# Cross-attention with image prompts: the last batch re-planned over eight PSUM banks, with a block diagonal prompt product

## The chip, the cores and the metric

The kernel runs on one core of a Trainium2 chip. The core has a matmul engine (TensorE, "PE" in the profile; its weight loads are "PEld"), a vector engine (VectorE, "DVE"), a scalar engine (ScalarE, "ACT"), a general engine (GpSimd, "POOL") and a queue that issues DMAs (SyncE, "SP"). PE writes into PSUM, a small memory of eight banks; DVE and ACT read it, POOL cannot. Each engine works through its own instructions in the order in which they are written, and engines wait for each other through semaphores. The metric is the device time of one execution in microseconds (us); lower is better. All arithmetic is fp32.

## What is computed

Eight batches; 112 queries of 320 channels each (20 heads of 16); a context of 375 tokens of 512 channels, of which the first 371 are text and the last 4 are image prompts. The reference, cut to what matters:

```python
text_ehs, ip_ehs = ehs[:, :-4], ehs[:, -4:]
q = heads(x @ W_q); k_t = heads(text_ehs @ W_k); v_t = heads(text_ehs @ W_v)
probs_t = softmax(q @ k_t.T * 0.25)                  # 112 x 371 per head
text_out = probs_t @ v_t
k_ip = heads(ip_ehs @ W_k_ip); v_ip = heads(ip_ehs @ W_v_ip)
qsem = l2norm(probs_t @ text_ehs)                    # 112 x 512 per head
sem = qsem @ l2norm(ip_ehs).T                        # 112 x 4
probs_ip = softmax(q @ k_ip.T * 0.25 + 0.5 * sem) * spatial_mask[:, None]
out = (text_out + probs_ip @ v_ip) @ W_out + b_out + x
```

The norm of `probs_t @ text_ehs` is the costly part. The kernel never forms that 112 x 512 product. It forms the Gram matrix of the context once per batch and needs, per head, the quadratic form of the probabilities with it.

## The kernel before, in words

**Groups.** The 20 heads of a batch b make five groups g of four heads. For one group, `multiplied` (L574) multiplies the transposed probabilities `xgT` of four heads with `u` on PE, in 12 steps j; the four heads use four row strips of PE at the same time. `u` holds the Gram matrix (half of it, doubled), the normalised prompts, a column of ones and, in its last 16 columns, the values of the group's heads. The result `ps_qd` is one PSUM bank per head: 371 columns of the Gram product, and 21 columns with the prompt products, the softmax sum and the text output.

**Around it.** `scores` (L528) makes one head's scores on PE into a bank `ps_s`. `probabilities` (L549) takes their negated maximum on DVE (`nmx`, L553), the exponential on ACT (`p`, L557) and sends p to `xg` by DMA (L560). `transposed` (L564) turns `xg` into `xgT` with one DVE instruction per group. `value_sums` (L597) copies the 21 columns to `pvs` on ACT. `reduced` (L626) multiplies the 371 columns with p and sums them on DVE (L630) into `ss`. `shared` (L602) does that for two of a group's four heads on ACT and POOL instead. `placed` (L502) copies the next group's values into `u` on POOL, in three pieces c; piece c may be written when PE has done the steps of the group in hand that read it. Scores are made two groups ahead (`LEAD`, L766).

**finish** (L643) ends a batch. It is a generator whose pieces are placed by hand between the groups of the next batch: `z`, `rn` (L672, L674); square root on ACT, then the table for Exp is loaded again (L677, L678), `zr` and the normalised text output `attn` (L680, L683); `fu`, the prompts' logits less their maximum (L688 to L694); `ex` (L698); `w`, the prompts' weights (L704 to L708); `wv`, the product of weights and prompt values `vip` on POOL, summed over four prompts and added to `attn` (L712 to L725); three transposes of `attn` into `ps_a` and the copy `aT` (L731, L735); the projection `ps_o` with W_out (L744); `ob`, the addition of x and bias (L753); the DMA to the output (L756). `ob` has one buffer. The last batch is finished in two parts, its first 16 heads (`first`) and its last four (`last`, with the sums on DVE, L720, L721).

**Other work between groups**, in `between` (L778): the Gram matrix, values, keys and queries of the next batches. `values` (L458) is 320 columns wide for the first and the last batch and 384 for the others, whose extra 64 columns are the keys of the last four heads, copied to `k3`; `keys` (L431) then makes its third block by three transposes of `k3` instead of four matmuls. `prompt_logits` (L510) makes `ps_ip`, the prompts' scores.

**PSUM.** Three pools share the eight banks: four for `ps_qd`, two for `ps_sc`, two for `ps_mm` (L78 to L80). `bank()` (L82) takes one of `ps_mm`, or of `ps_sc` with `spare`. A tile gets a bank when all readers of the bank's last tile are done.

**Order.** On PE, SP, DVE and ACT (and on POOL in the last batch) the instructions stand in the order of the program. The loop of L875 does batches 0 to 6, the loop of L930 the last batch, b = 7. What follows the loop (L974 to L985) interleaves the rest of batch 6 and the two parts of batch 7. `awake` (L364) gives PE matmuls whose results nobody reads. DMAs with tensors on chip are issued by SP, in order.

Of the kernel before, what the change touches and what calls it, by code (L numbers as in the profile page):

```python
# [20 lines left out]
def kernel(  # L21
# [174 lines left out]
    vipd = dram.tile([N, C], F32, tag="vipd", name="vipd", bufs=1)  # L196

# [233 lines left out]
    def keys(b):  # L431
        s = st[b]
        for i in range(NC):
            ps = bank(f"ps_k_{b}_{i}")
            if 0 < b < B - 1 and i == FULL:
# [22 lines left out]
    def values(b):  # L458
        s = st[b]
        ctxT, vext = s["ctxT"], s["vext"]  # L460
        w = C + REST if 0 < b < B - 1 else C
# [39 lines left out]

    def placed(b, g):  # L502

        s = st[b]
        for c in range(NT):
            nc.gpsimd.tensor_copy(  # L506
                region(b, c)[:, :, UV - c * P :], s["vr"][:, c * QN : (c + 1) * QN, g, :]
            )

    def prompt_logits(b):  # L510
        s = st[b]
        qT, _, j = queries[b]
        ps = bank(f"ps_ip_{b}", spare=b == B - 1)
# [14 lines left out]
    def scores(b, g, a, early=False):  # L528
# [6 lines left out]
        elif b == B - 1 and g > 1 and a < 2:  # L535

            ps = bank(f"ps_s_{b}_{g}_{a}")
        else:
            ps = ps_sc.tile([P, 512], F32, tag="sc", name=f"ps_s_{b}_{g}_{a}")
# [34 lines left out]
    def multiplied(b, g):  # L574
# [3 lines left out]
        for a in range(GROUP):  # L578

            if b == B - 1 and (g, a // 2) in ((NG - 2, 0), (NG - 1, 1)):  # L580
                banks.append(bank(f"ps_qd_{b}_{g}_{a}"))
# [15 lines left out]
    def value_sums(b, g):  # L597
        s = st[b]
        for h, ps in zip(groups[g], s["qd", g]):
            nc.scalar.copy(s["pvs"][:, h, :], ps[:S, TT:UW])  # L600

    def shared(b, g):  # L602
# [3 lines left out]
        if b == B - 1:  # L606
            t = work.tile([P, NE, TP], F32, tag="ctxT", name=f"shared_{b}_{g}")
            prods = [t[:S, a, :TT] for a, _ in some]
        else:

            t = work.tile([S, NIP, H, D], F32, tag="wv", name=f"shared_{b}_{g}", bufs=1)
            prods = [t.rearrange("p n h d -> p (n h d)")[:, a * TP : a * TP + TT] for a, _ in some]
        p = s["p", g]
        for a, (h, ps) in some:
            nc.scalar.copy(prods[a], ps[:S, :TT])
# [27 lines left out]
    def finish(b, heads=(0, H), eng=None, late=False, table=None):  # L643
# [55 lines left out]
        if table:  # L699
            nc.scalar.preload_act_table(table)  # L700
# [9 lines left out]

        wv = work.tile([S, NIP, H, D], F32, tag="wv", name=f"wv_{b}_{h0}", bufs=1)[:, :, :n]
# [16 lines left out]
        i0, i1 = h0 * D // P, -(-h1 * D // P)  # L728
# [11 lines left out]
        if not late:  # L740
            s["o"] = bank(f"ps_o_{b}", spare=b >= B - 2)
# [5 lines left out]
        if h1 < H:  # L747
            yield
            return
        yield  # L750

        ob = work.tile([S, C], F32, tag="ob", name=f"ob_{b}", bufs=1)
        nc.vector.tensor_tensor(ob, ps[:S, :C], s["xb"], ALU.add)  # L753
        yield

        nc.sync.dma_start(out[b], ob)  # L756
        del st[b]
# [20 lines left out]
    def between(b, g):  # L778
# [26 lines left out]
        if g == 3:  # L805
# [4 lines left out]
            run(("t", b), lambda: prompt_logits(b))  # L810
            if nb < B - 1:
# [5 lines left out]
        if g == 4:  # L817
# [6 lines left out]
            for bs in (first if b > 0 else []) + rest:  # L824
                run(("q", bs[0]), None)

# [48 lines left out]
    for n, (b, g) in enumerate(steps[:-NG]):  # L875
# [35 lines left out]
        if g == NG - 1:  # L911
# [17 lines left out]
    before = ("f", b - 1)  # L929
    for g in range(NG):  # L930
        coming = g + LEAD if g + LEAD < NG else None
        for j, _ in enumerate(multiplied(b, g)):
            for a in {0: (2, 3), 1: (0, 1)}.get(j, ()) if coming else ():
                scores(b, coming, a)
                probabilities(b, coming, a)
# [3 lines left out]
            if g == 2:  # L939
                run(before, lambda: finish(b - 1))  # L940
            if g == 3:
                nc.scalar.preload_act_table(AF.Sqrt)
            if g + 1 < NG:
                transposed(b, g + 1)
            if g == 2:
                run(before, None)
            if g == 3:
                run(before, None)
        value_sums(b, g)
        if g < LEAD + 1:  # L950
            sums = shared(b, g)
            next(sums)
            reduced(b, g, 2)
        else:
            reduced(b, g)
        if g + 1 < NG:
            placed(b, g + 1)
        if g < LEAD + 1:
            next(sums)
        if g == 0:  # L960
            run(("k", b), None)
            run(("f", b - 2), None)
        if g == 1:
            prompt_values(b)
        if g == 2:
# [63 lines left out]
```

## Time and profile before

| | us |
|---|---|
| median of 3 runs | 455.98 (454.32 to 457.4) |
| the profiled execution: device time | 457.81 |
| the profiled execution: span | 456.0 |
| PE busy, its share of the span | 440.5, 97% |
| DVE busy, its share | 312.5, 69% |
| first matmul of the last batch's five groups | 401.23, 409.27, 415.79, 424.35, 432.47 |
| the last `ob` ends | 453.02 |

How to read it: every row of a timeline has a start, a duration, an engine and a line; rows that follow each other are merged (x10). In brackets stands how long the engine had been idle before the row and who released it. Matmuls are pipelined, so what a matmul costs in a stream is read from the distance of two starts. An fp32 matmul of the program appears as two MATMUL rows, a transpose as one. Up to the start of the last batch PE has no gaps worth naming; the last 55 us are where PE, DVE, POOL and ACT wait for each other.

### The profile page before, as it was taken

To read this page: it belongs to the slowest core of one execution; us is meant where nothing else is said; L and a number is where in the kernel's file an instruction comes from. 1 tells how busy PE (TensorE), PEld (TensorE's weight loads), DVE (VectorE), ACT (ScalarE), POOL (GpSimd) and SP (SyncE) were. 2 spreads that over 40 slices of the span, in tenths; PEclk is the share of its full clock that TensorE was granted. 3 is DMA by queue.
4 is the path that set the end of the run, shared out by engine and by line. 5 is a ranking of instruction groups with operands and counts; after the bars stand their busy time and mean duration, and the time that the engine had idled before them with its cause. 6 is when DMAs were issued, how large, how long until landed. Compare 5 with 4: busy or idle time off the path is not lost.

```text
span 456.0 us, 12969 instructions
## 1 busy us (share of the span) xinstructions
PE 440.5 (97%) x5136; PEld 340.8 (75%) x5136; DVE 312.5 (69%) x657; ACT 190.4 (42%) x529; POOL 115.2 (25%) x264
## 2 busy tenths in 40 slices
PE   8998999999999999999999999999999999999885
PEld 8757867877678877887778877887768777877763
DVE  3047456786677668786676668787687668878883
ACT  2263233345344353345334353335335353356640
POOL 4302200102051114212061113312050213333490
PEclk9999999999999999999999999999999999999887
DMA  8679853645646454646645554545645455654100
GB/s 242 166 181 257 201 154 105 153 125 162 161 129 164 137 134 139 149 129 166 170 115 153 153 148 135 139 134 156 169 124 131 129 126 147 153 165 133 40 1 25
DMA packets 52069, 64.99 MB, mean 143 GB/s; under 512 B 18369, under 2 KB 43985, under 8 KB 52009
## 3 DMA queue, kind: packets, MB, share of 16 engines
q1 hardware_dynamic: 51568, 63.62, 52.5%
q8 instruction: 40, 0.66, 0.7%
q10 hardware_dynamic: 440, 0.56, 0.4%
q14 instruction: 21, 0.16, 0.1%
HBM read 19.46 MB, written 5.12 MB: 54 GB/s over the span
## 4 chain that ended last, share of the span: by engine, by line
PE 89%; DVE 3%; ACT 3%; issue 2%; DMA 1%; POOL 1%; SPq 0%; DVEq 0%; ACTq 0%; POOLq 0%
PE ps_qd L587 41%; PE ps_v L465 14%; PE ps_k L448 9%; PE ps_g L412 8%; PE ps_s L540 4%; PE ps_o L744 3%; PE ps_q L301 3%; PE ps_c L351 2%; PE ps_g L384 1%; PE ps_w L371 1%; ACT p L557 1%; DMA xg<-p 1%; PE ps_ip L517 1%; DVE xgT L568 1%; DMA ct<-in_ctx_dram 1%
## 5 line engine op out<-in xcount | busy, mean ns | idle before, releaser
L587 PE MATMUL ps_qd<-u,xgT 32*112 32x232 f32 (+11 forms) x3840 | 220.5, 354 | 4.4 <-POOL u L506 3.3
L587 PEld LDWEIGHTS ps_qd<-u,xgT 32*112 32x112 f32 x3840 | 185.1, 173 | 40.9 <-issue 9.5
L553 DVE TENSOR_REDUCE nmx<-ps_s 112x1 f32<-112x371 f32 x160 | 77.5, 528 | 75.6 <-PE ps_s L540 75.4
L568 DVE STREAM_TRANSPOSE xgT<-xg 128x1536 f32<-128x1536 f32 x40 | 118.9, 2973 | 4.8 <-DMA xg<-p 4.8
L557 ACT ACTIVATE p<-ps_s,nmx 112x371 f32<-112x371 f32 x160 | 82.5, 573 | 60.5 <-DVE nmx L553 48.1
L630 DVE CUSTOM_DVE_ANT_0 junk<-ps_qd,p 112x371 f32<-112x371 f32 x152 | 82.3, 542 | 18.3 <-ACT pvs L600 2.1
L506 POOL COPY u<-vr 128x64 f32<-128x64 f32 x120 | 26.0, 239 | 174.3 <-PE ps_qd L587 118.1
L540 PE MATMUL ps_s<-kT,qm 32*112 32x371 f32 x320 | 63.3, 476 | 0.4 <-ACT p L557 0.4
L465 PE MATMUL ps_v<-wv_sb,ctxT 128*128 128x384 f32 (+1 forms) x192 | 63.5, 480 | 0.0
L465 PEld LDWEIGHTS ps_v<-wv_sb,ctxT 128*128 128x128 f32 x192 | 35.2, 190 | 19.7
L448 PE MATMUL ps_k<-ctxT,wk_sb 128*128 128x371 f32 x144 | 48.7, 482 | 0.0
L600 ACT COPY pvs<-ps_qd 112x21 f32<-112x21 f32 x160 | 16.5, 189 | 66.6 <-PE ps_qd L587 66.5
L448 PEld LDWEIGHTS ps_k<-ctxT,wk_sb 128*128 128x128 f32 x144 | 26.5, 190 | 16.1 <-issue 0.5
L412 PE MATMUL ps_g<-ctxT 128*128 128x375 f32 (+2 forms) x168 | 37.4, 379 | 0.0
L412 PEld LDWEIGHTS ps_g<-ctxT 128*128 128x128 f32 x168 | 28.1, 190 | 8.4
L540 PEld LDWEIGHTS ps_s<-kT,qm 32*112 32x112 f32 x320 | 25.6, 170 | 5.0 <-ACT kT L455 2.1
L310 DVE TENSOR_SCALAR qm<-ps_q,emask 128x224 f32<-128x224 f32 (+1 forms) x25 | 9.2, 400 | 24.6 <-PE ps_q L301 24.5
L712 POOL TENSOR_TENSOR wv<-vip,w 112x1280 f32<-112x1280 f32 (+1 forms) x8 | 19.2, 2405 | 14.8 <-DVE w L708 14.6
L472 ACT COPY vext<-ps_v 128x384 f32<-128x384 f32 (+1 forms) x24 | 11.2, 466 | 27.1 <-PE ps_v L465 26.7
L455 ACT COPY kT<-ps_k 128x371 f32<-128x371 f32 x18 | 8.4, 469 | 28.9 <-PE ps_k L448 28.9
L744 PE MATMUL ps_o<-wo_sb,aT 128*112 128x320 f32 x48 | 16.4, 479 | 2.8 <-ACT aT L735 2.8
L400 ACT ACTIVATE ug<-ps_g 128x375 f32<-128x375 f32 (+2 forms) x24 | 9.0, 377 | 23.7 <-PE ps_g L412 20.6
(110 smaller groups left out, 324.1 us busy)
## 6 DMA issues: line engine op xcount, KB each, us to landing
xg<-p SPq DMA_DIRECT2D x160, 162.3 KB
u<-ug SPq DMA_DIRECT2D x128, 99.0 KB
vip<-vipd SPq DMA_DIRECT2D x8, 560.0 KB
ct<-in_ctx_dram SPq DMA_DIRECT2D x16, 256.0 KB
vr<-vd SPq DMA_DIRECT2D x32, 120.0 KB
vd<-vext SPq DMA_DIRECT2D x7, 320.0 KB
ct<-in_ctx_dram SPq DMA_DIRECT2D x8, 224.0 KB
vd<-vext SPq DMA_DIRECT2D x7, 160.0 KB
```

The lines of the kernel that those rows point to most:

```text
L412: nc.tensor.matmul(ps[:, : T - t0], ctxT[:, e, t0 : t0 + P], ctxT[:, e, t0:T], start=(e == 0), stop=(e == NE - 1),)
L448: nc.tensor.matmul(ps[:, :TT], wk_sb[:, e, i * P : (i + 1) * P], s["ctxT"][:, e, :TT], start=(e == 0), stop=(e == NE - 1),)
L465: nc.tensor.matmul(ps[:, :w], ctxT[:, e, c * P : (c + 1) * P], wv_sb[:, e, :w], start=(e == 0), stop=(e == NE - 1),)
L506: nc.gpsimd.tensor_copy(region(b, c)[:, :, UV - c * P :], s["vr"][:, c * QN : (c + 1) * QN, g, :])
L540: nc.tensor.matmul(ps[:S, :TT], qm[a * RG : (a + 1) * RG, i, r, j * S : (j + 1) * S], s["kT"][a * RG : (a + 1) * RG, i, :], start=True, st ...
L553: nc.vector.tensor_reduce(nmx, ps[:S, :TT], AX.X, ALU.max, negate=True)
L557: nc.scalar.activation(p, ps[:S, :TT], AF.Exp, bias=nmx)
L568: nc.vector.transpose(xT.rearrange("p j (k q) -> p q j k", q=QN), xg.rearrange("p q (j k) -> p q j k", k=RG),)
L587: nc.tensor.matmul(banks[a][:S, j * RG : UW], xT[a * RG : (a + 1) * RG, j, :S], region(b, c)[a * RG : (a + 1) * RG, q, q * RG :], start=(j ...
L630: nc.vector.tensor_tensor_reduce(out=junk, in0=ps[:S, :TT], in1=s["p", g][:, a, :], scale=1.0, scalar=0.0, op0=ALU.mult, op1=ALU.add, accu ...
L712: eng.tensor_tensor(wv, s["vip"][:, :, part], w.rearrange("p h n -> p n h").unsqueeze(3).to_broadcast([S, NIP, n, D]), ALU.mult,)
L744: nc.tensor.matmul(ps[:S, :C], aT[:, i, :], wo_sb[:, i, :], start=(i == 0), stop=(i == NC - 1))
```

## The change

1. **Batch 7's keys and values** follow the other batches: `values(7)` is 384 wide and the third key block is three transposes. These now stand in batch 6's group 3, where the other batches have theirs; the four matmuls of `ps_k` between groups 0 and 1 of the last batch go.
2. **`prompt_logits(7)`** moves from between groups 3 and 4 of the last batch to directly ahead of its group 0, behind the last `ps_q`.
3. **Banks and scores of the last batch.** The products of groups 1 to 4 and the scores for groups 2 to 4 change places among the three pools, so that the next tile takes a bank that comes free early. In groups 1 and 2 the scores of heads 0 and 1 are made at step j = 2 instead of j = 1. On ACT the two shared heads' copies come first (`pvs`, `shared`, `pvs`, `shared`), then the other two `pvs`.
4. **finish(6)** is later in its parts: its square root stands behind group 2's copies, its `fu` behind the transposition for group 4, its `w` behind group 3's reductions, and its transposes and projection behind group 4's products. `finish(7, first)` is re-ordered likewise: `ex` behind group 4's copies, `w` behind group 4's reductions.
5. **Prompt values by TensorE.** For batch 6 and for the first 16 heads of batch 7 the POOL work of L712 to L725 goes. The prompts' values are written once to DRAM as 80 rows (head, prompt) of 320 channels (`vipx`), loaded as `bd`, and two `affine_select`s on POOL zero the channels that are not the row's head, which makes a block diagonal matrix. `w` is transposed on PE (`wT`), and `ps_a` is the sum of `attn` times the identity and `bd` times `wT`, six matmuls for three transposes.
6. `awake(11)` becomes `awake(3)` and stands behind batch 6's projection; both `ob` additions stand at the end.

The diff, cut to its core:

```diff
+    vipx = dram.tile([2, H, NIP, C], F32, tag="vipx", name="vipx", bufs=1)
...
-            if 0 < b < B - 1 and i == FULL:
+            if b > 0 and i == FULL:
...
-        w = C + REST if 0 < b < B - 1 else C
+        w = C + REST if b > 0 else C
...
+    def prompt_values_by_head():
+        nc.sync.dma_start(vipx, vipd[N - 2 * NIP :, :].rearrange("(b n) c -> b n c", n=NIP)
+            .unsqueeze(1).to_broadcast([2, H, NIP, C]))
+    def load_prompt_values_by_head():
+        bd = io.tile([P, NT, E], F32, tag="ct", name="bd")[:HN, :2, :CP]
+        nc.sync.dma_start(bd[:, :, :C], vipx.rearrange("b h n c -> (h n) b c"))
+        return bd
+    def own_channels(bd):
+        nc.gpsimd.memset(bd[:, :, C:], 0.0)
+        v = bd[:, :, :C].rearrange("p b (h d) -> p b h d", d=D)
+        for sign, base in ((1, 0), (-1, NIP - 1)):
+            nc.gpsimd.affine_select(out=v, in_=v, compare_op=ALU.is_ge, fill=0.0, base=base,
+                pattern=[[0, 2], [-sign * NIP, H], [0, D]], channel_multiplier=sign)
...
-        ps = bank(f"ps_ip_{b}", spare=b == B - 1)
+        ps = bank(f"ps_ip_{b}")
...
-            if b == B - 1 and (g, a // 2) in ((NG - 2, 0), (NG - 1, 1)):
-                banks.append(bank(f"ps_qd_{b}_{g}_{a}"))
+            if b == B - 1 and (g, a // 2) in ((1, 0), (2, 1), (3, 1), (4, 1)):
+                banks.append(bank(f"ps_qd_{b}_{g}_{a}", spare=g == 3))
...
         for a, (h, ps) in some:                      # in shared()
+            if b == B - 1:
+                nc.scalar.copy(s["pvs"][:, h, :], ps[:S, TT:UW])
             nc.scalar.copy(prods[a], ps[:S, :TT])
...
+        if bd is not None:                           # in finish(), behind w
+            ps = ps_qd.tile([P, 512], F32, tag="qd", name=f"ps_wT_{b}")
+            nc.tensor.transpose(ps[: n * NIP, :S], w.rearrange("s h n -> s (h n)"), ident[:S, :S])
+            wT = work.tile([P, NE, TP], F32, tag="ctxT", name=f"wT_{b}")[:, 0, :S]
+            nc.scalar.copy(wT[: n * NIP], ps[: n * NIP, :S])
+            yield
+            ps = bank(f"ps_a_{b}_{h0}")
+            for i in range(i0, i1):
+                o = ps[:, i * S : (i + 1) * S]
+                nc.tensor.matmul(o, attn[:, i * P : (i + 1) * P], ident[:S, :S], start=True, stop=False)
+                nc.tensor.matmul(o, bd[: n * NIP, i * P : (i + 1) * P], wT[: n * NIP], start=False, stop=True)
...
-                run(("k", nb), None, 1)
+            if nb == B - 1:                          # end of between(6, 4)
+                run(("t", nb), lambda: prompt_logits(nb))
...
+        if (b, g) == (B - 3, 1): prompt_values_by_head()
+        if (b, g) == (B - 2, 1): bd = load_prompt_values_by_head()
-        if g == NG - 1:
+        if g == NG - 1 and b < B - 2:
             prompt_values(b)
...
+    places = {0: {0: (2, 3), 1: (0, 1)}, 1: {0: (2, 3), 2: (0, 1)}, 2: {0: (2, 3), 2: (0, 1)}}
     for g in range(NG):                              # the last batch
+        own = {}
+        for a in (0, 1) if g in places else ():
+            if g == 0: own[a] = bank(f"ps_s_{b}_{g + LEAD}_{a}")
+            elif g == 2: own[a] = ps_qd.tile([P, 512], F32, tag="qd", name=f"ps_s_{b}_{g + LEAD}_{a}")
...
+        if g <= LEAD:
+            sums = shared(b, g); next(sums); value_sums(b, g, 2); reduced(b, g, 2)
+        else:
+            value_sums(b, g)
+            if g == NG - 1:
+                run(before, None)                    # wT of batch 6
+                next(first)                          # ex of batch 7, first 16 heads
+                run(before, None)                    # ps_a and aT of batch 6
+                nc.scalar.preload_act_table(AF.Sqrt)
+                run(before, None)                    # ps_o of batch 6
+            reduced(b, g)
...
-        if g == 0:
-            run(("k", b), None)
         if g == 1:
             prompt_values(b)
+            own_channels(bd)
...
     last = finish(b, (FULL * HC, H), nc.vector, late=True)
-    run(before, None, 2)
-    awake(11, end=True)
-    for _ in range(3): next(last)
-    run(before, None)
-    next(first); next(last); next(first)
-    run(before, None)
-    drain(first); drain(last)
+    next(last)
+    next(first)                                      # w of the first 16 heads
+    next(last)
+    awake(3, end=True)
+    next(first)                                      # wT
+    for _ in range(2): next(last)                    # fu, ex of the last four heads
+    for _ in range(2): next(first)                   # ps_a, ps_o
+    for _ in range(4): next(last)
+    drain(gens[before]); drain(first); drain(last)
```

## The prediction

> **What bounds the kernel now.** I read the page's busy table and slices first.
>
> ```profile
> PE 440.5 (97%) x5136; PEld 340.8 (75%) x5136; DVE 312.5 (69%) x657; ACT 190.4 (42%) x529; POOL 115.2 (25%) x264
> ...
> PE   8998999999999999999999999999999999999885
> ...
> PEclk9999999999999999999999999999999999999887
> ```
>
> PE sets the time until the last batch; only the last slices have idle PE and a lower granted clock. So I then read the timeline of the last batch.
>
> ```profile
> 401.23 1.22 PE L587 MATMUL ps_qd<-u,xgT 32*112 32x392 f32 x10
> ...
> 401.70 0.25 ACT L313 COPY qT<-ps_q 128x112 f32<-128x112 f32 x1 [0.70 <-DVE qm L310]
> ...
> 404.62 3.03 DVE L568 STREAM_TRANSPOSE xgT<-xg 128x1536 f32<-128x1536 f32 x1
> ...
> 406.58 2.76 PE L448 MATMUL ps_k<-ctxT,wk_sb 128*128 128x371 f32 x8
> ...
> 409.27 1.22 PE L587 MATMUL ps_qd<-u,xgT 32*112 32x392 f32 x10
> ...
> 412.67 2.97 DVE L568 STREAM_TRANSPOSE xgT<-xg 128x1536 f32<-128x1536 f32 x1
> ...
> 415.79 1.57 PE L587 MATMUL ps_qd<-u,xgT 32*112 32x392 f32 x9 [1.09 <-DVE xgT L568]
> ...
> 417.44 0.85 POOL L668 TENSOR_TENSOR xb<-x_sb,bias_sb 112x320 f32<-112x320 f32 x1
> ...
> 423.37 0.74 POOL L683 TENSOR_TENSOR attn<-pvs,zr 112x320 f32<-112x320 f32 x1 [5.08 <-DVE zr L680]
> 424.06 0.58 POOL L506 COPY u<-vr 128x64 f32<-128x64 f32 x3
> ...
> 424.35 7.50 PE L587 MATMUL ps_qd<-u,xgT 32*112 32x392 f32 x96 [2.16 <-POOL u L506]
> ```
>
> Here DVE, not PE, paces. A group's products take PE 5.4 us (401.23 to 406.58). DVE waits 1.6 us for the first scores, takes their four maxima (about 1.9) and then transposes 3.0: the next `xgT` is there 6.4 us after the group's start, in both group 0 and group 1. In group 0 the `ps_k` matmuls fill the gap; ahead of group 2 PE idles 1.09, ahead of group 3 2.16, there for POOL, whose `u` stands behind `attn`, which waits for DVE's `zr`. Third, the stages of the end with busy times by engine (PE, PEld, DVE, ACT, POOL, how many instructions in brackets); the third number from the right is the granted clock. And the chain of waits:
>
> ```profile
> 424.30:426.40 2.10, 2.05 (x19) 1.42 (x23) 1.45 (x6) 1.24 (x7) 1.47 (x4) 1.00 0.03 8
> 426.40:429.80 3.40, 3.40 (x35) 3.38 (x31) 3.30 (x5) 1.66 (x6) 1.00 (x2) 0.50 0.01 2
> 438.00:440.00 2.00, 0.54 (x4) 0.30 (x3) 1.15 (x4) 1.61 (x4) 1.78 (x4) 1.00 0.00 0
> 440.00:446.90 6.90, 6.17 (x20) 4.86 (x21) 5.05 (x18) 2.17 (x7) 4.53 (x4) 0.51 0.02 7
> ```
>
> ```profile
> 438.63 1.28 ACT L700
> 439.93 0.41 ACT pvs L600 x4
> ...
> 440.73 3.54 PE ps_o L744 x6
> 444.27 3.75 PE ps_w L371 x22
> ...
> 448.50 0.23 ACT ex L698
> ...
> 452.53 0.49 DVE ob L753
> ```
>
> After each longer gap PE runs at half clock, for 3.4 and for 6.9 us. In the end the last four heads' `ex` waits for ACT's `aT`, thus for 22 slow matmuls of `awake`.
>
> **The change part by part**, against this execution (span 456.0, device time 457.81, the median 1.83 lower; I add the difference to the median).
>
> *Ahead of the last batch, PE-bound, so all of it counts.* Values: 8 matmul rows of 384 columns take 2.68 (328.82 to 331.50), of 320 columns 2.25 (379.02 to 381.27): +0.43 x 3 = **+1.29**. Third key block: three transposes, 0.36 in batch 5 (343.37 to 343.73), and a wait for the `kT` copy, which frees the bank: in batch 6 PE would be there at 392.33, the copy ends at 392.48: **+0.53** in all. `ps_ip`: six rows, 0.52 (391.81 to 392.33); but its third block needs the `qT` copy, which ended at 401.95 behind `qm`, while `ps_q` was issued by 401.13; group 0 is queued behind it on PE. Start of group 0 at about 402.2 instead of 401.23: **+1.0**. Group 0 so starts at 401.23 + 2.82 = 404.05. The two DMAs of the prompt values are two issues on SP (0.5 us, as `vip`'s) between issues of `xg` that wait for ACT anyway; uncovered they would cost 0.5 each. A DMA of `vip` goes as well.
>
> *Groups 0 to 2.* `ps_k` (2.69, and 0.52 of issue behind it) goes, but the next `xgT` is late instead: group 1 at 404.05 + 6.42 + 0.15 = 410.6 (before 409.27). ACT's reordered copies free both shared banks 1.1 us after group 0's end, by 410.5, in time; the DVE reductions that free the others end at 412.0, ahead of the scores at j = 2. Group 2 again 6.52 later: 417.15 (before 415.79). So the new banks take away little: DVE's order is as long as it was. Group 3: the 0.4 us that group 2's scores waited for a bank go; `xgT` ends at about 417.15 + 6.8 = 423.9. POOL: `attn` is behind the next `shared`, but memset and two selects come ahead of `xb` and `u`. The only row of a select is 0.29 for 128 columns, the lower end; POOL's 640-element product (1.56, L723) is the nearest row of that size, twice it the upper end. 0.29 x 5 = 1.46 lies at the product: I take 1.5 each. `shared` ends at 418.7; + 0.2 + 3.0 + 0.85 + 0.25 = 423.0: hidden behind `xgT`. From 2.0 each it shows; at 3.1 each group 3 starts 2.2 late, which costs the end 0.2, as PE has 1.9 to spare there (below). Group 3 at **424.05** (before 424.35): nearly all that was won is spent on the 2.82.
>
> *Groups 3, 4.* DVE now does two reductions and `xgT` ahead of `fu`: 423.9 + 1.6 + 2.95 + 1.35 = 429.8; on ACT `ex` 0.27 and the square root's table 1.28 stand ahead of group 3's `pvs`: 431.45; first reduction at 431.7 (before 431.94). PE may lose 1.9 here to half clock and still be in time. From there: four reductions, `z`, `rn` (to 434.6), `zr`, `sx`, `rx`, `w` (1.1 more), then `fu`, whose rows were 0.92, 0.90 and 0.65 beside POOL's `wv` work and 0.35, 0.24, 0.24 in the mean without: 437.2 (before 438.26). `pvs` of group 4 are no longer behind `ex` and a table load: reductions from **437.3** (before 440.13), 2.8 us won.
>
> *The end.* Three things take it back. (a) `ps_a` of batch 6 gets the bank of group 4's third head, so it waits for the third reduction: 439.3. `aT`, and behind `aT` on ACT the table for the square root, wait with it; before, that table was loaded early (L700). PE has idled 4 us and is at half clock: 12 rows at 0.19 (112/128 of the 0.214 between two slow `ps_w`; at full clock 0.10, by the 0.11 between two fast ones) + 0.3: 441.9; `aT` to 442.4; table 1.28, root, table 1.28: 445.2 (before 444.91). (b) PE: `ps_o` 3.33 as before, slow, six `ps_w` 1.28, `wT` 0.3, its copy on ACT 0.25: `ex` from 447.6 to 447.85 (before 448.72). (c) Behind `ex` DVE takes 2.16 to `attn`, as before, then batch 6's `ob` 0.49 (its bank is wanted by the last transpose); the last `ob` has to wait until that tile has been sent. Sending took from 453.02 to 455.04: 447.85 + 2.16 + 0.49 + 2.07 + 0.49 = 453.06, against 453.02. With the clock back at 445.5 (half of `ps_o` to `wT` 0.7 shorter) 452.4. I take 452.7: **−0.3**, and 455.98 − 0.3 = **455.7**.
>
> One rule weighs on this. Rows: PE idled 1.35 of the 3.4 us up to 426.4 and 1.3 of the 3.4 up to 440.0, and was halved after both; 1.09 of 412.7 to 416.1 left the clock alone. The Trainium skill, "TensorE: Matmul & The Clock Gate", section "Why this matters for your kernels", asks only for no gap above about 3 us. By it the new gaps of 1.1 to 1.45 us ahead of groups 1 to 3 are free; by the rows they lie at the edge. That is the slow rival below.
>
> **Rivals.**
> *PE stays warm at the end.* If the clock does not fall before 439.3 (its steps are 3.4 us apart, and the idle time began at 435.2): `aT` at 441.2, `ex` waits only for ACT's tables: 444.5. End 3.3 earlier, **452.6**. It decides where the 3.4 us steps fall: for it, one place in five; against it, 4 us of idle, twice what sufficed before. Only with a `ps_ip` that does not wait (1.0 less, which DVE hands on) does it come to 451.6, at the bound of 1% (451.4).
> *Slower: half clock in a group that makes scores.* Gaps of 1.2 ahead of group 1 and 1.1 ahead of group 2 now stand without `ps_k` as filler. It decides from somewhere between 1.09 and 1.3 us of idle PE in a 3.4 us stretch. A slow stretch brings that group's scores, and so DVE's whole order, 1.6 later (half of 3.4, less what falls behind the scores). One hit with the end at half clock throughout (last `ps_a` to `ps_o`, +1.5): 455.98 + 1.6 + 1.5 = **459.1**; two hits 460.7.
> *The banks do not do what they say*: scores wait for DVE as before, 0.4 once or twice: 456.3, the forecast's neighbourhood.
>
> **How the numbers follow.** No change as forecast: 0.48; banks that do nothing: 0.06. Warm end: 0.20, of which 0.13 with gains that no row shows, below 451.4. Slow stretches: 0.26, of which 0.19 with two hits or waits that no row shows, above 460.5. Measurement tells about 1% (4.6 us) from no change; so faster 0.13, same 0.68, slower 0.19. The range takes in the warm end and one hit (452.6, 459.1) and half a microsecond and one more for the prices bounded above: 452.0 to 460.0.
>
> **What would show it.** Right: group 0 starting near 404.05 behind a wait of `ps_ip` for `qT`; idle PE ahead of groups 1 and 2 for `xgT`; group 3 not waiting for `u`; group 4's reductions near 437; the square root's table load behind `aT` near 442; the last `ob` waiting for the output DMA. Wrong: `ps_a` of batch 6 starting before 438, selects of 3 us and more, or a half-clock stretch in groups 1 or 2.

## The result and the profile after

The changed kernel takes 458.41 us (median of 12 runs, 457.18 to 459.47) against 455.39 for the kernel before in the same comparison (454.18 to 459.35): ratio 1.0058, 95% interval 1.0033 to 1.0082. It is slower by more than the measurement leaves open, though by less than 1%; 455.7 had been forecast.

The two profiled executions don't show that: 457.81 us before, 458.18 after, 0.37 apart. So the first thing to look at is not where 3 us went, but why the medians differ by 3 and the profiles by 0.4. Every run comes with the mean granted TensorE clock of its span; a stretch of 3.41 us at half clock takes 0.0037 off it (half of 3.41, over a span of 456). All runs of the kernel before whose clock is listed (111, from four comparisons and one run of it as an experiment), and all 24 of the changed kernel, sorted by that clock:

| mean granted clock | before: runs, median us | after: runs, median us |
|---|---|---|
| 0.995 and more | 24, 454.4 | none |
| 0.992 to 0.994 | 36, 455.6 | none |
| 0.988 to 0.991 | 10, 456.6 | 14, 457.7 |
| below 0.988 | 41, 458.15 | 10, 458.1 |

The time of the kernel before goes in steps with the number of half-clock stretches, though not without exception: two runs of the first row took 457.2 and 457.3 us. (One run of the last row, 460.98 us, is on record as slow; without it the row's median is the same.) The profiled execution (457.81, two stretches of 3.4 and 6.9 us) was one of the last row; all 70 runs of the other rows are faster than it. Where the stretches lay is on record only for profiled executions. The changed kernel is in the two lower rows in every run, and its profile has one stretch of 3.41 and one of 6.83 us in the last batch.

The page of the changed kernel, share of the span in 40 slices (first PE's busy time, then the granted clock):

```profile
PE 438.3 (96%) x5132; PEld 339.7 (74%) x5132; DVE 308.8 (68%) x657; ACT 191.1 (42%) x531; POOL 107.7 (24%) x260
...
PE   8998999999999999999999999999999999998865
...
PEclk9999999999999999999999999999999999999879
```

Its timeline of PE alone in the last batch (start, duration, in brackets the idle time before and its releaser):

```profile
403.52 1.08 PE L549 MATMUL ps_ip<-kipb,qT 128*112 128x32 f32 x6
404.54 1.22 PE L617 MATMUL ps_qd<-u,xgT 32*112 32x392 f32 x10
...
411.08 1.22 PE L617 MATMUL ps_qd<-u,xgT 32*112 32x392 f32 x10 [1.11 <-ACT pvs L630]
...
418.11 1.22 PE L617 MATMUL ps_qd<-u,xgT 32*112 32x392 f32 x10 [1.41 <-DVE xgT L597]
...
425.53 11.09 PE L617 MATMUL ps_qd<-u,xgT 32*112 32x392 f32 x192 [1.79 <-DVE xgT L597]
437.29 0.27 PE L739 MATMUL ps_wT<-ident,w 112*80 112x112 f32 x1 [0.68 <-DVE w L733]
440.25 0.66 PE L749 MATMUL ps_a<-ident,attn 112*128 112x112 f32 x2 [2.69 <-DVE ss L657]
...
443.57 3.54 PE L767 MATMUL ps_o<-wo_sb,aT 128*112 128x320 f32 x6 [0.53 <-ACT aT L760]
```

`ps_a` of batch 6 waits 2.69 us for `ss`, DVE's third reduction of group 4, because it takes that head's bank. `ps_o`, behind it, takes 3.54 us; where the clock is full it takes 1.87. The windows of the same kernel (busy us by engine PE, PEld, DVE, ACT, POOL; granted clock third from the right) show the clock around the two longest gaps. It changes only at borders that lie 3.41 us apart (from 426.75 to 440.40 are four such steps); where a step without a change is named, here and below, its border is counted in steps from a change in the same execution:

```profile
423.34:426.75 3.41, 1.62 (x30) 1.24 (x27) 3.17 (x6) 3.36 (x11) 2.16 (x4) 1.00 0.55 153
426.75:430.16 3.41, 3.41 (x34) 2.71 (x31) 2.92 (x2) 1.96 (x5) 0.96 (x2) 0.50 0.01 2
436.99:440.40 3.41, 0.42 (x2) 0.27 (x3) 2.84 (x13) 1.48 (x7) 0.06 (x1) 1.00 0.00 0
440.40:447.23 6.83, 6.30 (x20) 4.72 (x21) 2.58 (x14) 3.21 (x4) 0.00 (x0) 0.50 0.00 0
```

PE is busy 0.42 of the 3.41 us before 440.40, and then runs at half clock until 447.23: nearly all of `ps_a` and `ps_o`. The chain of the changed kernel's end (start, duration, engine):

```profile
431.66 1.28 ACT L1026
432.95 0.19 ACT pvs L630
433.16 0.54 DVE junk L657
...
438.34 0.45 DVE junk L657
...
439.64 0.54 DVE junk L657
440.25 0.66 PE ps_a L749 x2
...
443.08 0.45 ACT aT L760
443.57 3.54 PE ps_o L767 x6
447.12 0.78 PE ps_w L373 x6
...
448.23 0.22 ACT ex L725
...
450.98 1.97 DMA out_dram<-ob
...
453.07 0.49 DVE ob L780
```

The chain goes from DVE's reductions through `ps_a`, `aT`, the slow `ps_o` and `awake` to the last four heads' `ex`, and the last `ob` waits for the output DMA.

### The profile page after: what moved, and what is told of

Read it like the earlier page. It is cut to its first block, busy times and chain, and to the rows that moved or that the text cites. A ratio compares the mean times of both kernels' runs of the same rounds, so it can differ in the third digit from the quotient of the medians.

```text
span 456.5 us, 12952 instructions
## 1 busy us (share of the span) xinstructions
PE 438.3 (96%) x5132; PEld 339.7 (74%) x5132; DVE 308.8 (68%) x657; ACT 191.1 (42%) x531; POOL 107.7 (24%) x260
## 5 line engine op out<-in xcount | busy, mean ns | idle before, releaser
L617 PE MATMUL ps_qd<-u,xgT 32*112 32x104 f32 (+11 forms) x3840 | 218.0, 353 | 5.5 <-DVE xgT L597 3.2
L467 PE MATMUL ps_v<-wv_sb,ctxT 128*128 128x384 f32 (+1 forms) x192 | 64.7, 487 | 0.0
L450 PE MATMUL ps_k<-ctxT,wk_sb 128*128 128x371 f32 x136 | 45.9, 482 | 0.0
L450 PEld LDWEIGHTS ps_k<-ctxT,wk_sb 128*128 128x128 f32 x136 | 25.1, 190 | 15.4 <-issue 0.5
L403 POOL TENSOR_TENSOR ug<-ug,half 128x128 f32<-128x128 f32 (+1 forms) x24 | 10.8, 453 | 29.6 <-ACT ug L402 29.6
L789 POOL TENSOR_TENSOR wv<-vip,w 112x1280 f32<-112x1280 f32 x6 | 14.8, 2462 | 11.4 <-DVE w L733 11.4
```

Of the source, the lines that this page charges most:

```text
L450: nc.tensor.matmul(ps[:, :TT], wk_sb[:, e, i * P : (i + 1) * P], s["ctxT"][:, e, :TT], start=(e == 0), stop=(e == NE - 1),)
L467: nc.tensor.matmul(ps[:, :w], ctxT[:, e, c * P : (c + 1) * P], wv_sb[:, e, :w], start=(e == 0), stop=(e == NE - 1),)
L617: nc.tensor.matmul(banks[a][:S, j * RG : UW], xT[a * RG : (a + 1) * RG, j, :S], region(b, c)[a * RG : (a + 1) * RG, q, q * RG :], start=(j ...
L789: eng.tensor_tensor(wv, s["vip"][:, :, part], w.rearrange("p h n -> p n h").unsqueeze(3).to_broadcast([S, NIP, n, D]), ALU.mult,)
```

## The experiments

The theory: the change by itself is worth nothing, as forecast, but it makes certain what happens to the kernel before only in some runs, half clock through the whole end. Rivals: a term of the sum is missing (the moved scores, the `ps_ip` ahead of group 0, the bank), or the medians of two comparisons differ for reasons that have nothing to do with either kernel.

### The same two kernels again

The kernel before, unaltered, as an experiment:

> The kernel before, once more, for the span and granted clock of each of its runs. In the two profiled executions the changed kernel's last ob ended 0.5 us later than the kernel before's (453.56 against 453.02), while the medians of 12 runs differ by 3.0. Gate theory: the profiled execution of before was one of its slow ones; its half-clock stretches (3.4 us in group 3, 6.9 us at the end) come and go from run to run, and most runs of before have less of them. Then spans range from about 452.5 to 457, and the mean granted clock goes with them: above 0.986 in runs below 455 us. Work theory: the clock is not it; runs of before at 454.3 us show the same mean clock of 0.986 as the profiled one.

456.39 us (455.54 to 459.24), ratio 1.0020 (0.9994 to 1.0046). The spread is there, and goes with the clock in eleven of the twelve runs: 455.5 to 456.0 at 0.993, 458.07 and 458.15 at 0.986; the twelfth took 457.27 at 0.996. The profiled execution took 455.56. The windows of this run around its own half-clock stretch:

```profile
423.41:426.83 3.42, 2.17 (x20) 1.54 (x24) 1.77 (x8) 2.43 (x7) 2.52 (x6) 1.00 0.20 60
426.83:430.24 3.41, 3.41 (x82) 3.41 (x75) 3.31 (x5) 1.79 (x6) 1.12 (x3) 1.00 0.01 2
430.24:433.65 3.41, 2.91 (x20) 1.63 (x22) 2.97 (x9) 1.29 (x6) 1.75 (x2) 1.00 0.00 0
433.65:437.06 3.41, 3.41 (x31) 2.88 (x27) 3.08 (x9) 0.77 (x2) 3.25 (x3) 0.50 0.02 5
437.06:446.00 8.94, 7.64 (x96) 6.53 (x91) 7.08 (x25) 4.50 (x10) 7.10 (x8) 1.00 0.00 0
```

The same 2.16 us of waiting for `u` ahead of group 3 is cut by a step's border at 423.41, 0.91 and 1.25 us, and the next step stays at full clock; the one stretch among these windows falls into the middle of group 4. From 437.06 to 446.00 the clock is full, and the timeline of PE shows the end as the forecast never had it:

```profile
439.68 0.51 PE L731 MATMUL ps_a<-ident,attn 112*128 112x112 f32 x3
441.46 1.87 PE L744 MATMUL ps_o<-wo_sb,aT 128*112 128x320 f32 x6 [1.28 <-ACT aT L735]
443.17 2.62 PE L371 MATMUL ps_w<-ident 128*128 128x128 f32 x22
```

`ps_o` 1.87 instead of 3.54, `ps_w` 2.62 instead of 3.96. The changed kernel, unaltered, in another comparison:

> The changed kernel again, unaltered, beside the kept-awake one on the same chip. Theory (PE idles over 2 us at its end in every run, so a half-clock stretch falls there in every run): 457.2 to 459.5 with no run below 456.5, clock never above 0.989. Rival (it wanders like the kernel before, whose medians were 455.4, 455.7 and 457.4 in three jobs): runs at 454 to 455 with a clock of 0.993 to 0.996 turn up.

457.94 us, 457.15 to 458.72, no clock above 0.989; the kernel before beside it 455.88 (454.21 to 459.75); ratio 1.0033 (1.0006 to 1.0060). Theory held. In one comparison the kernel before had a median of 457.38, since 16 of its 30 runs lay below 0.988: how much slower the change looks, between about half a microsecond (457.94 against 457.38) and 3 us, depends on how the kernel before falls.

### The clock taken away

13 matmuls whose results nobody reads, between `wT` and `ps_a` of batch 6:

```diff
             if g == NG - 1:
                 run(before, None)
                 next(first)
+                awake(13, end=True)
                 run(before, None)
```

> The changed kernel with 13 matmuls nobody reads (26 rows, 2.9 us at full clock) on PE between wT and ps_a of batch 6, where PE idles from 437.4 to 440.25. Gate theory: the clock stays up at the end, ps_a 1.2, ps_o 1.7 and ps_w 0.7 instead of 2.6, 3.5 and 1.0: ex about 2.5 to 3 us earlier, 2.5 us faster than the changed kernel, ratio to before 1.000. Bank theory alone (what counts is that ps_a waits for the reduction): no change, 1.006.

454.41 us (454.02 to 457.81), ratio 0.9970 (0.9945 to 0.9996), 4.0 below the changed kernel by medians of two comparisons, where 2.5 had been expected; clock 0.995 or 0.996 in every run. Again, beside the changed kernel on one chip:

> The kept-awake changed kernel again (13 matmuls behind wT), on the same chip as the changed kernel. Theory: 454.0 to 455.0, 3 to 4.5 us below the changed kernel of the same job. Rival (the 4.0 us between two jobs were the chips'): within 1.5 us of it.

455.01 (454.05 to 458.82) against 457.94, 2.9 us: a little less than the theory's 3, as three of the twelve runs took 457.2 to 458.8. The timeline of PE in the first of the two:

```profile
436.47 0.26 PE L739 MATMUL ps_wT<-ident,w 112*80 112x112 f32 x1 [0.72 <-DVE w L733]
436.57 3.08 PE L373 MATMUL ps_w<-ident 128*128 128x128 f32 x26
439.49 0.42 PE L749 MATMUL ps_a<-ident,attn 112*128 112x112 f32 x2
...
441.55 1.87 PE L767 MATMUL ps_o<-wo_sb,aT 128*112 128x320 f32 x6 [0.53 <-ACT aT L760]
```

`ps_a` starts no earlier against group 3 than in the changed kernel (14.8 us after its first matmul, there 14.7), and the end is 3 to 4 us earlier: adding work to PE won it. The same in the kernel before, nine such matmuls ahead of group 3 and eight between `ps_a` and `ps_o`:

```diff
+        for _ in range(9 if (b, g) == (B - 1, 3) else 0):
+            nc.tensor.matmul(banks[0][:, :P], ident, ident, start=True, stop=True)
...
-    run(before, None, 2)
+    run(before, None)
+    awake(8, end=True)
+    run(before, None)
     awake(11, end=True)
```

> The kernel before, with PE kept busy by matmuls that nobody reads in its two long gaps: nine ahead of the last batch's group 3 (the 2.16 us wait for u) and eight between ps_a and ps_o of batch 6 (the 1.3 to 2 us wait for aT). Theory (the times of the kernel before spread over 454 to 459 us because half-clock stretches follow these gaps, at places that change from run to run): median 454.0 to 454.8, granted clock 0.996 in most runs, spread under 1 us. Against the kept-awake changed kernel (454.4) it tells what the change is worth without the clock: nothing, within 0.5 us. Rival (the spread has another cause, such as DMAs): median 455.2 to 456.0 with a spread of 3 us as before.

455.65 us, 454.74 to 457.62, while the kernel before beside it took 457.38; ratio 0.9959 (0.9936 to 0.9982). The theory's numbers were missed: the median lies 0.85 above its bound, the clocks are 0.991 to 0.999, and the runs spread over 2.9 us, of which a single run makes 1.5. The rival's numbers (455.2 to 456.0, a spread of 3 us) were hit. Its reason, a cause other than the clock, is not shown by that, since the runs below 0.988, 16 of 30 without the filler, are gone; nor is it ruled out for what spread is left. What can be read from it: runs at 0.995 and more took 455.0 here, 454.4 in the kernel before, 454.4 and 454.9 in the kept-awake changed kernel. Without half clock at the end the two kernels are equal within about half a microsecond.

### How much idle time

The kept-awake changed kernel with 6 matmuls instead of 13:

> The kept-awake changed kernel with 6 instead of 13 matmuls behind wT, so that PE idles 0.72 us ahead of wT and some 1.6 us ahead of ps_a, 2.3 us in one stretch of 3.4 if both fall in it. Theory (1.3 us of idle time in one 3.4 us step halves the clock, 1.1 does not): half clock at the end in most runs, median 456.5 to 458.5, some runs at 454.4. Rival (only a gap near the whole 3.4 us matters): 454.2 to 454.8 in all runs.

455.06 us, ratio 0.9966 (0.9938 to 0.9994), clock 0.996 in 10 of 12 runs. The theory's threshold fell; the rival's number was missed by 0.3. The windows of the profiled run:

```profile
436.15:439.56 3.41, 1.62 (x13) 1.46 (x13) 2.97 (x11) 1.77 (x7) 0.34 (x1) 1.00 0.00 0
439.56:442.98 3.42, 2.76 (x16) 2.22 (x17) 1.85 (x11) 1.64 (x2) 0.00 (x0) 1.00 0.00 0
```

PE was busy for 1.62 us of the step up to 439.56, exactly as much as in the changed kernel's step up to 426.75, and the clock held here and fell there. So idle time in a step is not what decides, or not alone.

### The terms of the sum, one by one

The bank. `ps_a` of batch 6 from the pool whose banks come free with group 3:

```diff
-            ps = bank(f"ps_a_{b}_{h0}")
+            ps = bank(f"ps_a_{b}_{h0}", spare=b == B - 2)
```

> The changed kernel with ps_a of batch 6 in a bank of ps_sc instead of ps_mm, so that it need not wait for group 4's third reduction. Bank theory: ps_a starts behind wT's copy at about 438.2 instead of 440.25, aT, the square root's table and ps_o follow 2 us earlier; ex of the last four heads ends about 2 us earlier and the execution is 1.5 to 2.3 us faster than the changed kernel: a ratio to the kernel before of about 1.001. Gate theory besides: PE has then idled less than 1.5 us ahead of ps_a, the clock may stay up through ps_o, another 1 to 1.5 us. If neither matters, the time of the changed kernel, 1.006.

455.29 us (453.55 to 457.51), ratio 0.9995 (0.9970 to 1.0021): 3.1 below the changed kernel by medians of two comparisons. `ps_a` started at 436.75, its part with `wT` at 437.62, instead of 440.25, and the runs fell into two heaps, 453.6 to 454.4 (clock 0.990 to 0.992) and 456.1 to 457.5 (0.985 to 0.992). The wait was real, and in the profiled execution (453.96) part of the half clock went with it: `ps_a` runs at full clock, `ps_o` still takes 3.49. The two heaps overlap in clock, so the clock's mean alone doesn't tell them apart.

`ps_ip` of batch 7 behind group 0 instead of ahead of it:

```diff
-            if nb == B - 1:
-                run(("t", nb), lambda: prompt_logits(nb))
...
         if g == 0:
+            run(("t", b), lambda: prompt_logits(b))
```

> The changed kernel with ps_ip of batch 7 between groups 0 and 1, where PE idles 1.1 us for xgT, instead of ahead of group 0, where it waits for the copy of qT. By the prediction's step group 0 starts 1.0 us earlier and hands that on through DVE's order to groups 1 to 4 and to the end, less up to 0.3 for the bank that ps_ip takes ahead of group 1: 0.7 to 1.0 us faster than the changed kernel, ratio to before about 1.004. If groups 1 to 4 don't follow, no change: 1.006.

457.52 us, ratio 1.0050 (1.0030 to 1.0069), 0.4 to 0.9 below the changed kernel's medians. The profiled execution (459.23) is the slowest of the twelve: it had a half-clock stretch far ahead, at 49.5 us, which makes all its starts late, and one of 10.3 us at the end. Distances can be read: group 0 starts 0.75 us behind the first `ps_q` matmul (403.70 to 404.45), with `ps_ip` ahead 1.82 (402.99 to 404.81 in the next experiment), and the groups follow at 6.53, 7.05 and 7.45, as in the changed kernel. So the term is 1.1 us and is handed on to group 3; the median shows less of it.

The scores of heads 0 and 1 at j = 1 again, in the kept-awake kernel:

```diff
-    places = {0: {0: (2, 3), 1: (0, 1)}, 1: {0: (2, 3), 2: (0, 1)}, 2: {0: (2, 3), 2: (0, 1)}}
+    places = {0: {0: (2, 3), 1: (0, 1)}, 1: {0: (2, 3), 1: (0, 1)}, 2: {0: (2, 3), 1: (0, 1)}}
```

> The kept-awake changed kernel, with the scores of heads 0 and 1 in groups 1 and 2 at step j = 1 again, as in group 0. Theory (the move to j = 2 makes DVE wait 0.33 us between its pairs of maxima in each of the two groups, and it paces): the distances of the first matmuls, group 1 to 2 and group 2 to 3, fall from 7.02 and 7.43 to 6.6 and 7.0; median 453.4 to 453.9, that is 0.6 to 1.0 us below the kept-awake one (454.4). Rival (the banks are not yet free at j = 1, so that PE waits for DVE there instead): the distances stay within 0.1 us, median 454.2 to 454.6.

455.58 us (453.88 to 457.52), ratio 0.9962 (0.9934 to 0.9990): no gain. Group 1 to 2 fell from 7.02 to 6.65 us, as expected; group 2 to 3 rose from 7.43 to 7.58.

The runs fell into two heaps here too, six at 453.9 to 454.7 us and six at 456.5 to 457.5, though eleven of the twelve have a clock of 0.995 or 0.996. The profiled execution (457.35) is one of the upper heap:

```profile
425.58 9.45 PE L617 MATMUL ps_qd<-u,xgT 32*112 32x392 f32 x192 [1.96 <-DVE xgT L597]
437.73 0.38 PE L739 MATMUL ps_wT<-ident,w 112*80 112x112 f32 x1 [2.69 <-DVE w L733]
437.90 4.56 PE L373 MATMUL ps_w<-ident 128*128 128x128 f32 x26
```

It has one half-clock stretch ahead of the last `ob`, like the kept-awake kernel's profile, but in another place. There (425.0 to 428.4) it lay in the products of groups 3 and 4, which took 11.09 us, and PE still had to wait 0.72 for `w`: that stretch cost nothing. Here the products take 9.45, PE waits 2.69 for the same `w`, and the stretch (437.56 to 440.97) falls on the filler, 4.56 instead of 3.08; `ps_a` starts 16.7 us after group 3's first matmul instead of 14.8. So the mean clock tells how many stretches a run had, and not what they cost. Whether the other runs of 457.2 to 457.8 us at 0.995 or 0.996, two of the kernel before and two of the kept-awake one, are of this kind is not shown; no profile of them was kept.

In the lower heap there is no gain either (454.4, as without the edit). The reason shows more plainly in the next kernel, which has all mendings so far: bank, `ps_ip`, scores, four and two matmuls of filler, and batch 6's `ob` ahead of the last four heads' `w`.

```diff
                 next(first)
+                awake(4, end=True)
                 run(before, None)
                 nc.scalar.preload_act_table(AF.Sqrt)
+                awake(2, end=True)
                 run(before, None)
...
+    run(before, None, 2)                       # ob of batch 6, ahead of w
```

> The changed kernel with all mendings together: bank of batch 6's ps_a from the other pool (no wait for group 4's third reduction), four and two matmuls that nobody reads behind wT and behind ps_a of batch 6 to keep the clock, ps_ip of batch 7 behind group 0, scores at j = 1, and batch 6's ob ahead of the last four heads' w, so that the last ob need not wait for its DMA. Theory (these five are separate terms of the sum): 454.4 less 2 (bank), 0.9 (ps_ip), 0.7 (scores) and 0.3 to 0.5 (ob): 450.0 to 451.0, below both kernels by over 4 us. Rival (they hide behind each other, the end being set by ACT's two table loads or by the clock): 452.5 to 453.5.

453.52 us (452.91 to 455.04), ratio 0.9915 (0.9884 to 0.9946). Better than both kernels, but the rival's number, not the theory's. Its timeline, first DVE, then POOL:

```profile
419.59 0.19 DVE L699 SCALAR_TENSOR_TENSOR z<-pvs 112x20 f32<-112x20 f32 x1
419.81 0.73 DVE L701 TENSOR_TENSOR rn<-ss,z 112x20 f32<-112x20 f32 x1
420.47 2.94 DVE L597 STREAM_TRANSPOSE xgT<-xg 128x1536 f32<-128x1536 f32 x1
```

```profile
419.62 0.88 POOL L695 TENSOR_TENSOR xb<-x_sb,bias_sb 112x320 f32<-112x320 f32 x1
```

`rn`, 0.18 us elsewhere, ends when POOL's addition ends (in the scores experiment it took 0.74). The scores had come earlier, and DVE met POOL. The last `fu` of batch 6 met the second `xb` in the same way (0.72 instead of 0.24). The other thing: `w` came 2.53 us after group 4's products, and the clock fell at 436.09.

### What sets the wait for w

In the chain above, the reductions of group 3 stand behind ACT's `pvs`, and those behind batch 6's `ex` and the table load of L1026: DVE idles 1.83 us there. The next kernel lets `pvs` go first, and moves POOL's work: the selects behind group 0, both `xb` to where DVE transposes or reduces. A further edit, which its expectation does not count, loads the last square root's table on ACT ahead of batch 6's `ps_a` and `aT` instead of behind them.

```diff
             if g == 3:
-                run(before, None, 2)           # fu and ex of batch 6, at j = 2
-                nc.scalar.preload_act_table(AF.Sqrt)
+                run(before, None)              # fu alone
...
             value_sums(b, g)
+            if g == 3:
+                run(before, None)              # ex, behind group 3's copies
+                nc.scalar.preload_act_table(AF.Sqrt)
...
                 next(first)
+                nc.scalar.preload_act_table(AF.Sqrt)
                 awake(4, end=True)
                 run(before, None)
-                nc.scalar.preload_act_table(AF.Sqrt)
                 awake(2, end=True)
...
         if g == 0:
+            own_channels(bd)                   # was at g == 1
...
         if g == 2:
             run(before, None)
+            st[b]["xb"] = work.tile([P, NE, TP], F32, tag="ctxT", name=f"xb_{b}")[:S, 0, :C]
+            nc.gpsimd.tensor_tensor(st[b]["xb"], x_sb[:, b, :], bias_sb, ALU.add)
```

> The mended kernel again, with three more things: the additions of x and bias and the two selects on POOL moved to where DVE makes no sum of two tensors (rn took 0.73 instead of 0.18 us and the last fu 0.72 instead of 0.23 while POOL's addition ran); group 3's copies of pvs on ACT ahead of ex and of the square root's table, so that the first reduction of group 3 needn't wait 1.8 us. Theory: group 2 to 3 takes 7.0 instead of 7.44 us, the reductions of group 3 begin 1.8 to 2.2 us earlier, w is there before group 4's products end, so the 2.53 us of idle PE ahead of wT go and the clock holds; 450.5 to 451.5 us, 2 to 3 below the mended kernel without them (453.5). Rival (the two table loads now stand where those copies stood and delay group 4's copies instead, or the clock falls all the same): 452.8 to 454.

449.32 us (448.81 to 450.19), ratio 0.9862 (0.9829 to 0.9895), 8.6 us below the changed kernel of the same comparison and 6.6 below the one before. Better than the theory's 450.5. Its timeline of all engines:

```profile
420.08 0.18 DVE L698 TENSOR_TENSOR rn<-ss,z 112x20 f32<-112x20 f32 x1
...
428.17 0.41 ACT L630 COPY pvs<-ps_qd 112x21 f32<-112x21 f32 x4 [1.17 <-PE ps_qd L617]
...
429.51 0.54 DVE L657 CUSTOM_DVE_ANT_0 junk<-ps_qd,p 112x371 f32<-112x371 f32 x1
...
433.64 0.27 PE L736 MATMUL ps_wT<-ident,w 112*80 112x112 f32 x1 [0.15 <-DVE w L730]
...
436.84 1.87 PE L764 MATMUL ps_o<-wo_sb,aT 128*112 128x320 f32 x6 [0.24 <-ACT aT L757]
...
444.24 0.49 DVE L777 TENSOR_TENSOR ob<-ps_o,xb 112x320 f32<-112x320 f32 x1 [2.19 <-PE ps_o L817]
```

The first reduction of group 3 comes at 429.51 (431.57 without these moves), PE waits 0.15 us for `w` instead of 2.53, the clock is full until 446.6, behind the last `ob`, and the last `ob` waits for PE, as in the kernel before this one, and not for a DMA. The edits were not run one by one, but the traces part them: group 2 to 3 takes 6.99 instead of 7.44 us (POOL's work), and the first reduction of group 3 comes 6.13 instead of 8.02 us after the group's first matmul (`pvs`). The table's move had little to win: in the kernel without it ACT was through with its tables at 443.11, 0.12 after PE had made the `wT` that ACT copies next. What of the rest is the clock and what the wait for `w` was not parted. Whether the filler is still needed:

> The kernel with all mendings, without the six matmuls that nobody reads behind wT and ps_a of batch 6. PE then idles some 1.1 us between wT and ps_a (434.65 less 433.75, and the filler's share) and some 0.9 between ps_a and ps_o, about 2 us in all, split over two steps of 3.4. Theory (with w there before group 4 ends, what is left of the gaps is too little to halve the clock, so the filler is not what won): 449.0 to 449.8 us, the clock at 0.995 or above. Rival (the filler keeps the clock): 451 to 453 in most runs, clock 0.990 to 0.993.

450.62 us (448.79 to 451.20), ratio 0.9862 (0.9821 to 0.9903). Between the two: two of six runs at 448.8 and clock 0.998, four at 450.5 to 451.2 and 0.996. The profiled execution (450.75) is one of the four, and has a stretch at half clock that holds `ps_o` (3.31 us). In such runs the filler would be worth some 1.5 us (against the 449.32 of another comparison); the rest, some 7 us against the changed kernel (458 to 450.6), does not need it.

## Why the prediction was wrong

**The step that failed** is the one ahead of the sum: "against this execution (span 456.0, device time 457.81, the median 1.83 lower; I add the difference to the median)". It takes the 1.83 us by which the profiled execution lay above the median as something that both kernels have. It was the price of a half-clock end; only 41 of the kernel before's 111 runs have a clock as low as that execution's. The sum then carried the same half-clock end into the changed kernel, where the clock is 0.989 or less in all 24 runs. Against its own execution the forecast of −0.3 stands beside a measured +0.37. The measured 3.02 us between the medians are these 0.37, the 2.42 by which the kernel before's profiled execution lies above its median of 455.39, and the 0.23 by which the changed kernel's lies below its own. So of the 2.7 us between 455.7 and 458.41 about 0.7 are terms of the sum, below, and 2 the baseline (1.83 and 0.23). The prediction weighed the position of the steps only for the changed kernel ("PE stays warm at the end", one in five; by the clocks it happened in no run), and never asked whether the fences that it showed, half clock after 426.40 and 440.00, were the rule for the kernel before. Its three times, 454.32, 455.98 and 457.4, with a profile above all of them, were the hint.

The terms, against the changed kernel's profile:

| step | predicted | measured |
|---|---|---|
| group 0 starts | 404.05, `ps_ip` behind `qT` | 404.54; 404.14 in the mean of seven profiled runs with this order |
| group 1, after group 0 | 6.55 | 6.54 |
| group 2, after group 1 | 6.55 | 7.03 |
| group 3, after group 2 | 6.90 | 7.42 |
| two selects | 3.0, hidden | 2.09, hidden: `u` not waited for |
| first reduction of group 3 | 431.7 | 433.16 |
| first reduction of group 4 | 437.3 | 438.26 |
| `ps_a` of batch 6 | 439.3 | 440.25 |
| `ex` of the last four heads | 447.6 | 448.23 |
| the last `ob` ends | 452.4 to 453.06 | 453.56 |

- *Ahead of the last batch* right: 2.82 predicted; 404.14 less 401.24 (mean of three runs of the kernel before, 401.23, 401.55 and 400.93) is 2.9.
- *Groups 0 to 2* mis-sized by 0.5 us twice. "The DVE reductions that free the others end at 412.0, ahead of the scores at j = 2" was right, but the second pair of scores at j = 2 comes 0.33 us after DVE wants it, in both groups. The rows in the changed kernel's timeline:

```profile
412.74 1.00 DVE L582 TENSOR_REDUCE nmx<-ps_s 112x1 f32<-112x371 f32 x2 [0.40 <-PE ps_s L569]
...
414.06 1.00 DVE L582 TENSOR_REDUCE nmx<-ps_s 112x1 f32<-112x371 f32 x2 [0.33 <-PE ps_qd L617]
```

  At j = 1 the 0.33 went from group 1 to 2 (6.65). I had taken the kernel before's 6.4 us for DVE's order although the change moves two of its four inputs.
- *Groups 3, 4*: the mechanism right (`ex` and a table load ahead of `pvs`), the time carried 1.5 us of lateness from above; 0.5 of it came back by group 4. That the wait for `pvs` could be had back, and with it the wait for `w`, the prediction didn't see.
- *The end* right: (a) the bank, (b) half clock, (c) the output DMA, each as written, 0.5 to 0.9 late from above.
- *The slow rival* named the right cause at the wrong place: no half-clock stretch fell in groups 1 or 2. Its idle threshold was wrong as well: 1.41 us of idle time in the step up to 419.92 left the clock alone. One of the two readings behind it is off, too: of the 3.4 us up to 440.0 PE was idle 1.46, not 1.3 (1.46 of the 2.00 in the window shown).

The Trainium skill, "TensorE: Matmul & The Clock Gate", Part 1, says that the window in which activity is watched runs freely, that the same kernel therefore has more or fewer slow matmuls at its start from run to run, and that the penalty of this warm-up is below 1% of a typical span. Here what differs from run to run lies mainly at the end; it is 0.8% (454.4 to 458.15), of the size that the page gives for the start, and more than the change itself.

## What to carry to other kernels

Before a sum is made against a profiled execution, place that execution among the kernel's runs, and ask which of its costs come in every run; a change is compared with the distribution and not with the one run that was drawn. Where PE waits near the end of a kernel, the price is the wait and the half clock behind it: mend the wait first (here one bank from the other pool, and four small copies ahead of a table load), and put filler matmuls only into what is left. A slow stretch cost nothing where PE would have waited anyway (groups 3 and 4) and about half its length where all else waited for PE (1.67 us on `ps_o`), so look at what it falls on. An edit that makes an engine earlier can push it into another's way: look at both after each step.

## What the runs showed of the hardware that was not expected

- The clock's steps are 3.41 us apart and their place differs from run to run, so that the same 2.16 us wait halves the clock in one run and not in the next. Idle time in the step does not decide alone: 1.79 us left it alone in the kernel with six filler matmuls, and 1.66 us in the scores experiment (before 427.33), while 1.01 us halved it in the last kernel without filler, and 0.50 in the first experiment (the step up to 433.65). The profile doesn't show what the gate counts, and no run was made for it; it stays open.
- DVE's sums of two tensors in on-chip memory wait for a POOL addition in progress: `rn` 0.73 us instead of 0.18, `fu` 0.87 and 0.72 instead of 0.24; transposes, maxima and the reductions from PSUM did not (in the last kernel with filler a transpose beside a POOL addition took 2.98, a reduction 0.54, as elsewhere). The Trainium skill, "SBUF — State Buffer", "Who interferes with whom", states it so: a vector instruction with two inputs in on-chip memory shares a read port with GpSimd. The runs agree.
- Two selects over 80 x 640 elements took 2.09 us together, 1.05 each, between the prediction's two ends of 0.29 and 3.1.
